# A four-layer image network on one core: a fixed order for the attention's keys, bounded scores in the linear attention, and gate scores from raw tokens

## The chip, the cores and the metric

The kernel runs on one core of one Trainium2 chip, in float32, as one launch. The metric is the device time of that core in microseconds (us). The kernel before was run three times: 7568.02 us is the median, 7562.25 the lowest and 7576.92 the highest.

The core has five engines that each run their own stream of instructions. In the profile they are PE (the matrix engine; PEld is its loading of weights), DVE (vector), ACT (activation functions), POOL (GpSimd) and SP, which here only issues transfers. Transfers (DMA) between the device memory and the on-chip memory run beside them. An engine waits for another on semaphores. Matrix products land in PSUM, [...]from which ACT or DVE copies ("evicts") them.

## What is computed

The input is 8 images of 56 x 56 pixels with 128 channels. Four layers follow one another; tokens are the 3136 pixels of an image.

```python
x = conv_layer(x)                  # layer 0: deformable convolution, layer norms, MLP
x = whiten(x)                      # layer 1: channels decorrelated by a 64 x 64 matrix
t = x.reshape(8, 3136, 128)
# layer 2: 8 heads of 16, keys = queries = values = h
h = ln(t) @ W_k.T
t = t + softmax(h @ h.T / 4) @ h @ W_o.T          # per image and head
t = t + ffn(ln(t))
# layer 3: linear attention, 4 heads of 32
q, k, v = split(ln(t) @ w_in.T)
q = softmax(q, over the 32 of a head) / sqrt(32)
k = softmax(k, over all 25088 tokens)             # one softmax for each channel
ctx = k.T @ (v / N)                               # per head, 32 x 32
t = t + ln((ctx applied to q) @ w_out.T + b_out) * ln_w
t = t + ffn(ln(t))

def ffn(x):                        # 64 experts, each picks 8 tokens of each image
    logits = x @ gate_w.T + gate_b                # [3136, 64]
    probs = softmax(logits, over the tokens)
    vals, idx = top_k(probs of each expert, 8)
    pooled = sum of the 8 chosen tokens, weighted by vals
    out = gelu([pooled, 1] @ weight1), then [.., 1] @ weight2
    return scatter_add(out * vals at idx)
```

`ln` subtracts a token's mean over its 128 channels and multiplies by one over the root of its variance plus a small constant.

## The kernel before

An image's 3136 tokens are worked in 28 tiles of 112 tokens (T = 112, NT = 28), four tiles to a group (GT = 4, 448 columns, QC), seven groups to an image (NG = 7), so 56 groups over all images. Channels lie on 128 partitions where a matrix is "transposed" (names with a T), tokens lie on partitions otherwise. Everything runs in the order of the functions that `token_layers` (L2223) calls, after layers 0 and 1.

*Weights* (L2241 to L2274). Weight matrices are loaded and transposed on PE. `gate_weights` (L2210) does this for the two gates, those of layer 2 and layer 3.

*`attention_keys`* (L1038) works image by image. It loads the tokens (L1061), stores them by token into `tok` (L1062), makes mean and variance of each tile (`bn_stats` and `bn_aggr` on DVE, L1066 and L1067) and one over the root with `rsqrt` (L1134: an addition on DVE at L1139, a power on POOL at L1140). It normalizes each tile on DVE (`xn`, L112), transposes it on PE (L121) and copies the transposed group with ACT (L122) into `xT`. Fourteen products `p_h` (L1082) give the keys, evicted by turns by ACT (L1086) and DVE (L1090) into `kT`; 25 products `p_v` (L1097) give the values, evicted into `va` (L1105, L1107). Keys and values are stored in device memory. A last step squares the values on POOL (`sq`, L1116) and reduces them on DVE (L1118, L1119), for a bound of all scores. Its instructions are ordered by the framework's scheduler, which picks for each engine among what is ready.

*`query_bound`* (L2079) makes a bound of layer 3's query scores from the norms of 128 rows of weights: `low3` is its negative and `small3` a flag that says whether it is below a limit (`SMALL3`, 40). A similar flag, `small`, chooses between `attend` and a version for large scores. Both flags are read into registers (`values_load`) before a branch.

*`attend`* (L1154) is layer 2's attention and the longest part, with an order written out by hand. Scores `p_s` (L1251), exponentials (L1259) and products with the values (L1304) run over blocks of queries. When a block's sums `acc` are complete, `finish` (L1343) divides them, multiplies by `wo_pad` on PE (L1374), adds the tokens (L1385), makes statistics (L1390), normalizes, transposes (`p`, L1411) and makes the gate scores `pr` (L1416). `finish` is a Python generator: each `yield` is a place where its issue pauses and other work is put in. Behind the last scores, at L1489 to L1497, the generators still open are advanced, two of them (`later[:2]`) in turn. `choose` (L1654) then picks the 8 best tokens of each expert from `pr`.

*Experts of layer 2* (`run_experts`, L2314) follow.

*`context_sums`* (L1947) is the softmax of layer 3's keys, over all tokens, times the tokens themselves. `pipeline` (L1934) advances one generator per group by one `yield` in each turn and starts a new group each turn, so several groups are in flight in different phases. A group's statistics come from `group_stats` (L2013); `minus_mean` (L2024) makes `ms`, and `scale_shift` (L2030) normalizes with four ACT instructions (L2033). Then the group is transposed, the keys `p_k` are made by channel, the running maximum over the groups so far is updated (`ntop`, L1983 to L1985), the factor by which the old sums fall is made (`fall`, L1987), the exponentials (`eT`, L1992) are transposed back on PE (`p_e`, L1997), copied by DVE (`e`), and multiplied with the tokens (`p_x`, L2002); `tot` and `den` (L2004, L2005) take the group in.

*`context_weights`* (L2038) turns the sums into one 128 x 128 matrix `cw`.

*`linear_layer`* (L2106) has a similar pipeline over the 56 groups: queries `p_q` and their exponentials `q`, the sum over each head `m` (DVE, L2146) and the division (POOL, L2148), a transposition, the product `p_y` with `cw` (L2155), its squares (ACT, L2161), one over the root of their mean (L2165 on DVE, L2166 on POOL), `y` (DVE, L2169), the addition to the tokens (POOL, L2172), and, for the feed-forward part, statistics, `ms`, normalization on ACT, a transposition (`nT`) and the gate scores (`p_g`, L2187). After the seventh group of an image, `choose` runs in the same pipeline. `context_sums` and `linear_layer` are ordered by the scheduler. The experts of layer 3 end the kernel.

Of the kernel before, what the change touches and what calls it, by code (L numbers as in the profile page):

```python
# [8 lines left out]
F32 = mybir.dt.float32  # L9
I32 = mybir.dt.int32  # L10
# [1027 lines left out]
def attention_keys(tc, k, w, yv, tok, kT_out, va_out, low, small):  # L1038
# [5 lines left out]
    n_b = yv.shape[1]  # L1044
    with ExitStack() as ctx:
        cp = ctx.enter_context(tc.tile_pool(name="akc", bufs=1))
        bp = ctx.enter_context(tc.tile_pool(name="akb", bufs=2))
        ps = ctx.enter_context(tc.tile_pool(name="akp", bufs=6, space=PSUM))
        vas = []
# [8 lines left out]
        for n in range(n_b):  # L1058
            t_sb = bp.tile([T, NT, C], F32, name="t")
            for h in range(2):  # L1060
                nc.sync.dma_start(t_sb[h * IW : (h + 1) * IW], yv[h, n])  # L1061
            nc.sync.dma_start(tok[n].rearrange("(t p) c -> p t c", p=T), t_sb)  # L1062
# [5 lines left out]
            rs = rsqrt(nc, k, bp, mv, NT)  # L1068
            xT = bp.tile([C, S], F32, name="xT")
            for g in range(NG):  # L1070
                xn = bp.tile([T, GT, C], F32, name="xn")
                for i in range(GT):
                    normalize(nc, xn[:, i], t_sb[:, g * GT + i], mv, rs, g * GT + i)
                transpose_group(
                    nc, k, ps, "m", xT[:, g * QC : (g + 1) * QC], xn, nc.scalar.copy
                )
            kT = bp.tile([128, 2, S], F32, name="kT", bufs=1)
            for g in range(2):
                for c in range(NG):
# [5 lines left out]
                    if c % 2:  # L1085
                        nc.scalar.activation(  # L1086
                            kT[:, g, cols], p, AF.Identity, bias=w.one16, scale=DK**-0.25
                        )
                    else:
                        nc.vector.tensor_scalar(  # L1090
                            kT[:, g, cols], p, DK**-0.25, w.one16, ALU.mult, ALU.add
                        )
                nc.sync.dma_start(kT_out[n, g], kT[:, g])
            va = vas[n % 2]
# [15 lines left out]

            sq = bp.tile([128, 2 * KT * 4, DK], F32, name="sq", bufs=1)
            v = va.rearrange("p g t j d -> p (g t j) d")[:, :, :DK]
            nc.gpsimd.tensor_tensor(sq, v, v, ALU.mult)  # L1116
            top = bp.tile([128, 2 * KT * 4], F32, name="top")
            nc.vector.tensor_reduce(top, sq, AX.X, ALU.add)  # L1118
            nc.vector.tensor_reduce(tops[:, n : n + 1], top, AX.X, ALU.max)  # L1119
# [1267 lines left out]
```

## Time and profile before

| part of the profiled execution | us from the span's start |
|---|---|
| layers 0 and 1, weights | 0 to 1515 |
| `attention_keys` | 1520 to 1869 |
| `attend`, all engines in full work | 1869 to 6397 |
| `attend`, its end | 6397 to 6480 |
| experts of layer 2 | 6480 to 6663 |
| `context_sums` | 6656 to 6909 |
| `linear_layer` | 6915 to 7345 |
| experts of layer 3 | 7345 to 7566 |
| span of the profiled execution | 7566.5 |
| its time | 7568.32 |
| median of three runs | 7568.02 |

The profile is of one execution, and the runs show how far another may lie from it. The whole span has PE busy 6499.5 us (86%), DVE 5210.3 (69%), ACT 4198.0 (55%) and POOL 2941.4 (39%). Such shares are averages over stages with different limits, so a stage is read from its own stretch of the timeline. In a line of the timeline stand start, duration, engine, line of the code, operation, output and inputs with their shapes, how many instructions were drawn together, and in square brackets how long the engine was idle before and what it waited for.

### The profile page before, as it was taken

The numbers are of one execution on the slowest core, as the hardware profiler recorded it, in microseconds if no ns is written. First come the engines' busy times: TensorE is split into PE (matmuls) and PEld (weight loads), VectorE is DVE, ScalarE is ACT, GpSimd is POOL, SyncE is SP. The second block draws the span as 40 slices with busy tenths as digits, with TensorE's granted clock in tenths as the row PEclk, the third lists the DMA queues.
The fourth block names the chain that finished last, engine by engine and source line by source line (L and its number), as shares of the span: only waits on it lengthen the run. The fifth ranks groups of instructions, "written<-read, shape, count | busy, mean of one in ns | idle before, by whom it ended". The sixth has DMA issues, their size and how long they took to land. (4 is left out here: it accounts for less than half of the span.)

```text
span 7566.5 us, 158564 instructions
## 1 busy us (share of the span) xinstructions
PE 6499.5 (86%) x60063; PEld 2893.4 (38%) x60063; DVE 5210.3 (69%) x9787; ACT 4198.0 (55%) x6563; POOL 2941.4 (39%) x2557
## 2 busy tenths in 40 slices
PE   7859999656999999999999999999999999556764
PEld 5646666433333323323323323323333323245542
DVE  7866664366677777777777777777777777356761
ACT  5634444222766666666666666666666665156750
POOL 0011111122544444444444444444444444333763
PEclk9968989866999999999999999999999999789776
DMA  6544343476888778778778778778778777544544
GB/s 162 163 101 88 85 87 63 155 224 202 198 202 205 188 187 205 190 185 205 192 186 205 189 185 206 187 189 205 191 186 206 187 185 170 202 109 125 134 132 139
DMA packets 737876, 1287.44 MB, mean 170 GB/s; under 512 B 119042, under 2 KB 504452, under 8 KB 730308
## 3 DMA queue, kind: packets, MB, share of 16 engines
q1 hardware_dynamic: 726868, 1260.77, 65.9%
q0 software_dynamic: 6144, 12.60, 0.6%
q8 instruction: 486, 7.96, 0.5%
q10 hardware_dynamic: 4080, 3.68, 0.2%
q14 instruction: 298, 2.44, 0.1%
HBM read 286.04 MB, written 197.81 MB: 64 GB/s over the span
## 5 line engine op out<-in xcount | busy, mean ns | idle before, releaser
L1259 ACT ACTIVATE e<-p_s 128x768 f32<-128x768 f32 (+2 forms) x3712 | 2887.7, 830 | 1577.2 <-PE p_s L1251 1312.7
L1297 POOL COPY x<-sq 32x1152 f32<-32x1152 f32 x1792 | 2062.4, 1151 | 2008.8 <-PE p_s L1251 1240.1
L1270 DVE STREAM_TRANSPOSE sq<-e 128x768 f32<-128x768 f32 x2688 | 2433.8, 950 | 516.7 <-ACT e L1259 267.0
L1251 PE MATMUL p_s<-q,kT 32*128 32x384 f32 (+2 forms) x14848 | 1893.4, 547 | 41.1 <-ACT e L1259 23.3
L1304 PE MATMUL av<-e,va 128*32 128x384 f32 (+2 forms) x14848 | 1644.2, 515 | 13.5 <-DVE acc L1327 8.5
L1304 PE MATMUL avx<-x,va 128*32 128x384 f32 x10752 | 1129.5, 492 | 57.5 <-issue 36.9
L1251 PEld LDWEIGHTS p_s<-q,kT 32*128 32x128 f32 (+1 forms) x14848 | 649.9, 180 | 1265.8 <-issue 836.1
L1304 PEld LDWEIGHTS av<-e,va 128*32 128x32 f32 (+1 forms) x14848 | 293.6, 108 | 1028.7 <-issue 938.6
L1304 PEld LDWEIGHTS avx<-x,va 128*32 128x32 f32 x10752 | 351.8, 111 | 635.8 <-issue 597.4
L616 POOL TENSOR_TENSOR rs<-rs,mhalf 112x4 f32<-112x4 f32 x112 | 116.0, 1036 | 786.2 <-DVE rs L615 786.2
L1323 DVE TENSOR_TENSOR acc<-acc,avx 128x384 f32<-128x384 f32 x336 | 183.7, 547 | 232.3 <-PE avx L1304 227.7
L121 PE MATMUL p_tr<-ident,xn 112*128 112x112 f32 x672 | 132.9, 337 | 184.0 <-DVE xn L112 138.3
L1140 POOL TENSOR_TENSOR rs<-rs,mhalf 112x4 f32<-112x4 f32 (+2 forms) x136 | 167.9, 1235 | 243.6 <-DVE ntop L1985 123.9
L532 ACT COPY wT<-p_w 88x448 f32<-88x448 f32 x152 | 138.1, 923 | 197.8 <-PE p_w L530 159.4
L2033 ACT ACTIVATE xn<-t,ms,rs 112x128 f32<-112x128 f32 x448 | 185.2, 487 | 73.8 <-DVE ms L2026 73.7
L644 PE MATMUL p_f<-x1T,w 128*128 128x448 f32 x448 | 206.1, 584 | 4.4 <-DVE x1T L639 2.8
L121 PEld LDWEIGHTS p_tr<-ident,xn 112*128 112x128 f32 x672 | 97.3, 167 | 278.2 <-issue 184.9
L530 PE MATMUL p_w<-ident,wide 112*88 112x112 f32 x896 | 144.6, 300 | 62.7 <-DMA px<-strips 37.8
L1393 POOL TENSOR_TENSOR rs_b<-rs_b,mhalf 128x3 f32<-128x3 f32 (+1 forms) x72 | 58.5, 815 | 352.8 <-DVE rs_b L1392 350.2
L327 DVE SCALAR_TENSOR_TENSOR acc<-xp,dw,acc 128x3136 f32<-128x3136 f32 x48 | 166.5, 3470 | 37.6 <-ACT acc L322 37.3
L628 DVE TENSOR_TENSOR y<-y,p_rs 128x448 f32<-128x448 f32 x112 | 69.2, 618 | 176.7 <-PE p_rs L621 176.6
L122 ACT COPY xT<-p_tr 128x448 f32<-128x448 f32 x112 | 59.6, 532 | 224.8 <-PE p_tr L121 198.7
(366 smaller groups left out, 7904.0 us busy)
## 6 DMA issues: line engine op xcount, KB each, us to landing
x<-sq SPq DMA_DIRECT2D x5376, 144.0 KB
w<-in_L_ffn_weight_dram SPq DMA_DIRECT2D x64, 1024.0 KB
px<-strips SPq DMA_DIRECT2D x64, 616.0 KB
va_d<-va SPq DMA_DIRECT2D x16, 1600.0 KB
xT_d<-xT SPq DMA_DIRECT2D x112, 224.0 KB
xT<-xT_d SPq DMA_DIRECT2D x112, 224.0 KB
kT_d<-kT SPq DMA_DIRECT2D x16, 1568.0 KB
t<-t_a SPq DMA_DIRECT2D x16, 1568.0 KB
```

The costliest lines, as they stand in the source:

```text
L121: nc.tensor.transpose(p[:, i, :], src[:, i, :], k.ident[:T, :T])
L327: nc.vector.scalar_tensor_tensor(acc, xp[:, j // 3 : j // 3 + IH, j % 3 : j % 3 + IW], dw[:, j : j + 1], acc, ALU.mult, ALU.add,)
L530: nc.tensor.transpose(p[:, g], around[:, :, g], k.ident[:T, :T])
L644: nc.tensor.matmul(p, q.w1[:, f * 128 : (f + 1) * 128], x1T, start=True, stop=True)
L1140: nc.gpsimd.tensor_tensor(rs, rs, k.mhalf[:m, :n], ALU.pow)
L1251: nc.tensor.matmul(ss[j // 2][:m, j % 2, :width], kT[rows, 128 * i : 128 * i + m], q[rows, :width], start=True, stop=True,)
L1259: nc.scalar.activation(e[:m, 2 * j : 2 * j + 2, :width], ss[j][:m, :, :width], AF.Exp)
L1270: nc.vector.transpose(sq[:, :, i, j : j + 2].rearrange("p s j c -> p j s c"), exps[u, b, a, i][:, j : j + 2, :QB].rearrange("p j (s c) -> ...
L1297: nc.gpsimd.tensor_copy(*moves.pop(0))
L1304: nc.tensor.matmul(out, keys[u, b][1][:m, i, j, :], e[j], start=start, stop=stop)
L1323: nc.vector.tensor_tensor(to, to, in_order(av), ALU.add)
L2033: nc.scalar.activation(out[:, i], x[:, i], AF.Identity, bias=ms[:, i : i + 1], scale=rs[:, i : i + 1])
```

## The change

Six things are changed.

1. `attention_keys` gets an order written out by hand (`manual_schedule`: each engine runs its instructions in the order of the program). A tile's partitions become half and row of the image, with 28 pixels of the row in one partition, so that a load or store moves 14336 bytes in one piece instead of 512. The statistics of the next image are a generator that is advanced between the key products. ACT evicts all keys. The transposed group is copied into `xT` at places 28 columns apart. The squares and reductions of an image are issued in the next one.
2. At the end of `attend` all open generators are advanced in each round, three such rounds begin while the last squares are still being worked, and the buffers that several blocks need at once are the score squares' or more in number.
3. `context_sums_bounded` is new. Instead of the running maximum it subtracts the bound; it has an order written out by hand, makes keys by token, and sums in one PSUM tile over all groups. A column of ones beside the tokens gives the denominators. The flag `small3` chooses between it and the old function.
4. `query_bound` becomes `score_bound`, over 256 rows (queries and keys), and stands ahead of the weights.
5. In `linear_layer` the gate scores are made from tokens that are not normalized, by token, and multiplied by one over the root of the variance; then they are transposed.
6. For that, the gates' weights are centred: each row's mean is subtracted, so that a token's mean adds nothing. This is done for both gates.

```diff
-def attention_keys(tc, k, w, yv, tok, kT_out, va_out, low, small):
+def attention_keys(tc, k, w, y, tok, kT_out, va_out, low, small):
...
+        def statistics(n):
             t_sb = bp.tile([T, NT, C], F32, name="t")
-            for h in range(2):
-                nc.sync.dma_start(t_sb[h * IW : (h + 1) * IW], yv[h, n])
-            nc.sync.dma_start(tok[n].rearrange("(t p) c -> p t c", p=T), t_sb)
+            inner = tok[n].rearrange("(h f i) c -> f h i c", f=2, i=NT)
+            for f in range(2):
+                of = slice(f * IH, (f + 1) * IH)
+                nc.sync.dma_start(t_sb[of], y[:, n, f * NT : (f + 1) * NT])
+            yield
+            for f in range(2):
+                nc.sync.dma_start(inner[f], t_sb[f * IH : (f + 1) * IH])
...
             for i in range(NT):
                 nc.vector.bn_stats(st[:, i], t_sb[:, i])
                 nc.vector.bn_aggr(mv[:, i], st[:, i])
-            rs = rsqrt(nc, k, bp, mv, NT)
+                if i % GT == GT - 1:
+                    yield
+            stats[n] = t_sb, mv, rsqrt(nc, k, bp, mv, NT)
...
+        for n in range(n_b):
+            t_sb, mv, rs = stats.pop(n)
+            if n + 1 < n_b:
+                ahead.append(statistics(n + 1))
+                advance(ahead)
...
+                p = ps.tile([C, GT, 2, IH], F32, tag="m", name="p_tr")
+                for i in range(GT):
+                    nc.tensor.transpose(
+                        p[:, i].rearrange("c f h -> c (f h)"), xn[:, i], k.ident[:T, :T]
+                    )
+                nc.scalar.copy(by_place[:, g * GT : (g + 1) * GT], p)
+            advance(tail)
...
                         p, wk[:, g * 128 : (g + 1) * 128], xT[:, cols], start=True, stop=True
                     )
-                    if c % 2:
...
+                    advance(ahead)
+                    nc.scalar.activation(
+                        kT[:, g, cols], p, AF.Identity, bias=w.one16, scale=DK**-0.25
+                    )
```

The end of `attend`, and the scores' bound:

```diff
+        ending = True
+        rooms = [room()]
+        early = 3
         while jobs:
             keep_squares()
+            if early:
+                go_on_all()
+                early -= 1
             from_squares()
-        for work in urgent:
-            go_on(work)
-        ending = True
+            while urgent:
+                go_on(urgent.pop(0))
+        while urgent:
+            go_on(urgent.pop(0))
+        rooms.append(room())
         while later:
-            for work in later[:2]:
-                go_on(work)
+            go_on_all()
...
-def query_bound(tc, k, w, w_in, low, small):
+def score_bound(tc, k, w_in, low, small):
...
-        raw = bp.tile([C, C], F32, name="raw")
-        nc.sync.dma_start(raw, w_in[:C])
+        raw = bp.tile([C, 2, C], F32, name="raw")
+        nc.sync.dma_start(raw, w_in[: 2 * C].rearrange("(a p) c -> p a c", p=C))
```

The new function for the context sums, from its first yield on, with the branch:

```diff
+            rs, mv = group_stats(nc, k, wp, t)
+            yield
+            ms = minus_mean(nc, wp, rs, mv)
+            xn = wp.tile([T, GT, C + 1], F32, name="xn", bufs=6)
+            nc.gpsimd.memset(xn[:, :, C:], 1.0)
+            for i in range(GT):
+                if i % 2:
+                    nc.scalar.activation(xn[:, i, :C], t[:, i], AF.Identity, ...)
+                else:
+                    nc.vector.tensor_scalar(xn[:, i, :C], t[:, i], ...)
+            yield
+            p = ps.tile([C, GT, T], F32, tag="m", name="p_tr")
+            for i in range(GT):
+                nc.tensor.transpose(p[:, i], xn[:, i, :C], k.ident[:T, :T])
+            xT = wp.tile([C, QC], F32, name="xT")
+            nc.scalar.copy(xT, p.rearrange("c a t -> c (a t)"))
+            nc.sync.dma_start(xT_out[n][:, g * QC : (g + 1) * QC], xT)
+            yield
+            p = ps.tile([T, GT, C], F32, tag="m", name="p_k")
+            for i in range(GT):
+                nc.tensor.matmul(p[:, i], xT[:, i * T : (i + 1) * T], w.w_in[:, C : 2 * C], ...)
+            e = wp.tile([T, GT, C], F32, name="e")
+            nc.scalar.activation(e, p, AF.Exp, bias=low[:T])
+            yield
+            for i in range(GT):
+                nc.tensor.matmul(sums, e[:, i], xn[:, i], ...)
...
-        context_sums(tc, k, w, t_a, xT_d, tot, den)
+        with tc.If(taken > 0) as both:
+            context_sums_bounded(tc, k, w, low3, *sums)
+        with both.Else():
+            context_sums(tc, k, w, *sums)
```

The linear layer and the gates:

```diff
-            rs, mv = group_stats(nc, k, wp, t)
-            yield
-            ms = minus_mean(nc, wp, rs, mv)
-            xn = wp.tile([T, GT, C], F32, name="xn")
-            scale_shift(nc, xn, t, rs, ms)
+            rs, _ = group_stats(nc, k, wp, t)
+            tT = wp.tile([C, QC], F32, name="tT")
+            transpose_group(nc, k, ps, "m", tT, t, nc.scalar.copy)
...
-            nT = wp.tile([C, QC], F32, name="nT")
-            transpose_group(nc, k, ps, "m", nT, xn, nc.scalar.copy)
+            p = ps.tile([T, GT, E], F32, tag="m", name="p_g")
+            for i in range(GT):
+                nc.tensor.matmul(
+                    p[:, i], tT[:, i * T : (i + 1) * T], gate_w, start=True, stop=True
+                )
+            sc = wp.tile([T, GT, E], F32, name="sc")
+            nc.vector.tensor_tensor(
+                sc, p, rs.unsqueeze(2).to_broadcast([T, GT, E]), ALU.mult
+            )
             yield
-            p = ps.tile([E, QC], F32, tag="m", name="p_g")
-            nc.tensor.matmul(p, gate_w, nT, start=True, stop=True)
+            p = ps.tile([E, GT, T], F32, tag="m", name="p_sc")
+            for i in range(GT):
+                nc.tensor.transpose(p[:, i], sc[:, i], k.ident[:T, :T])
...
+    mean = rp.tile([E, 1], F32, name=name + "_m")
+    nc.vector.tensor_reduce(mean, raw, AX.X, ALU.add)
+    nc.vector.tensor_scalar(mean, mean, 1.0 / C, None, ALU.mult)
+    nc.vector.tensor_scalar(raw, raw, mean, None, ALU.subtract)
```

## The prediction

> **What bounds the kernel now.** I read the slices of the page first, then a table of busy time by stretch with the bounds of each stage (columns: stretch, its length, then busy time of PE, PEld, DVE, ACT and POOL, granted clock, DMA share, GB/s), then the timeline of one repetition of each stage.
>
> ```profile
> PE   7859999656999999999999999999999999556764
> PEclk9968989866999999999999999999999999789776
> ...
> 1532.70:1868.90 336.20, 200.79 (x854) 133.25 (x854) 226.58 (x820) 85.69 (x200) 78.25 (x16) 0.71 0.66 217
> 1869.00:6397.00 4528.00, 4364.20 (x41547) 1429.55 (x41547) 3423.48 (x4905) 2922.62 (x3818) 2145.24 (x1890) 0.98 0.80 194
> 6410.90:6455.00 44.10, 23.11 (x85) 14.36 (x85) 25.53 (x78) 0.00 (x0) 4.28 (x5) 0.65 0.14 41
> 6656.00:6909.00 253.00, 169.90 (x1008) 122.92 (x1008) 172.17 (x841) 167.47 (x448) 62.20 (x62) 0.92 0.38 104
> 6915.00:7345.00 430.00, 285.75 (x1580) 210.71 (x1581) 316.74 (x1160) 303.13 (x1016) 279.91 (x264) 0.77 0.54 142
> 1598.00:1606.00 8.00, 0.00 (x0) 0.00 (x0) 5.03 (x12) 0.00 (x0) 3.18 (x2) 0.50 1.01 421
> ```
>
> The main part of `attend` takes 4528 us with PE busy for 4364 of them: full, and its code unchanged. The four other stretches (keys, end of `attend`, context sums, linear layer) have no full engine. Each is a chain that passes from engine to engine, and all of the change is there. The keys of one image show such a chain, with the first tokens still to be loaded:
>
> ```profile
> 1564.13 4.80 POOL L1140 TENSOR_TENSOR rs<-rs,mhalf 112x28 f32<-112x28 f32 x1
> 1569.50 7.00 DVE L112 TENSOR_SCALAR xn<-t,mv,rs 112x128 f32<-112x128 f32 x27
> 1578.16 11.18 PE L1082 MATMUL p_h<-xT,wk 128*128 128x448 f32 x26
> 1589.17 5.89 PE L1097 MATMUL p_v<-wkT,xT 128*128 128x128 f32 x50
> ```
>
> POOL's power, DVE's normalizing, PE's keys and values come one after another; normalizing begins at 1532.7 for the first image and the last value copy ends at 1853.1: 320.4 us, a period of 42.1 us an image after 25.7 for the first.
>
> [...] the granted clock is 0.50 in 1574 to 1580 and 1.00 from 1582 on, and 0.71 over the stage. [...] `ms` takes 0.86 us in the linear layer, where POOL is busy, and 0.16 in the context sums.
>
> **Keys.** The new order makes the statistics of image n+1 while image n's keys are multiplied. DVE per image: 28 normalizations x 0.256 = 7.2 us; the deferred reductions 3.48 + 0.35 = 3.9; 28 pairs of statistics. In a fixed order each pair waits for itself; the end of `attend` shows it (first two rows before's keys, last two there):
>
> ```profile
> 1520.57 0.26 DVE L1066 BATCH_NORM_STATS2 st<-t 112x6 f32<-112x128 f32 x1
> 1520.83 0.26 DVE L1066 BATCH_NORM_STATS2 st<-t 112x6 f32<-112x128 f32 x1
> ...
> 6418.06 0.29 DVE L1390 BATCH_NORM_STATS2 st<-t 128x6 f32<-128x128 f32 x1
> 6418.49 0.26 DVE L1390 BATCH_NORM_STATS2 st<-t 128x6 f32<-128x128 f32 x1
> ```
>
> About 0.39 us a pair instead of 0.26: 28 x 0.39 = 10.9. The square of the values is 5.5 on POOL and is now beside DVE. The load of n+1 stands on SP's queue behind n-1's value stores: 3.3 MB at 421 GB/s (the last stretch above) is 7.8 us, [...]: it lands about 13 us after the image began. From there 10.9 + the add 0.3 + POOL 4.8 + handovers put the next image's first normalization at 29 to 30. PE's own path is 7.2 + 1.6 + 14 x 0.75 [...] + 5.9 = 27[...]. ACT now has all 14 key copies (14 x 0.63 = 8.9) and strided copies at 0.93 (like L558's 128x448 copy; 0.53 contiguous): 15.4 + value copies, inside 30. So a period of 30 (26.5 if the load lands early [...], 34 if it is late): 7 x 30 + 26 = 236 against 320.4, -84. Behind the stage two loads of flags go (1865.1 to 1868.9 holds them) as the bound moves ahead of the weights, -3; the bound's own chain there costs +1. **-86** (-110 to -58). Centring both gates is six small operations in that preparation, inside the +1.
>
> **End of `attend`.** From the last `acc` (6410.9) to the last `pr` (6455.0) pass 44.1 us with DVE busy 25.5: five blocks finish two by two. Now all go on in each step, and three early rounds take some of it beside the last squares. That moves about 10 us of DVE's 25.5 ahead, leaving 15.8 + some 5 of stalls; PE's order then lets output matmuls stand before the last `avx` until DVE has transposed, +9. 15.8 + 5 + 9 = 29.8: **-15** (-22 to -6). The square tiles it re-uses are free by then, so no store waits.
>
> **Context sums.** 55 periods from 6676.4 to 6904.5: 4.15 us, 4.25 in the steady part. What goes: the maximum 0.61, its two helpers, the copy of `e` 0.68, `tot` 0.32, `den` 0.20 on DVE; `fall` 0.29 and half of the 4 x 0.41 normalizations on ACT; 4 transposes (0.65) on PE. What comes: two normalizations on DVE (0.52), a `memset` on POOL, keys as four matmuls of 128 columns (about 1.1). What stays is a loop that a fixed order lays bare:
>
> ```profile
> 6673.60 0.15 DVE L1139 TENSOR_SCALAR rs<-mv 112x4 f32<-112x4 f32 x1
> 6673.83 1.01 POOL L1140 TENSOR_TENSOR rs<-rs,mhalf 112x4 f32<-112x4 f32 x1 [1.07 <-DVE rs L1139]
> 6674.87 0.16 DVE L2026 SCALAR_TENSOR_TENSOR ms<-mv,rs 112x4 f32<-112x4 f32 x1 [0.79 <-POOL rs L1140]
> ```
>
> From `rs` to `ms` 1.27 us. In program order DVE waits there with the next group's statistics behind it: 0.16 + 0.52 + 4 x 0.39 + 0.16 + about 1.2 = 3.6 a group. PE's turn is 1.16 + 1.1 + 0.55 + 0.45 = 3.3, ACT's 0.82 + 0.53 + 0.65 = 2.0. So (4.25 - 3.6) x 56 = -36, and +3 for the second pair of branches (flag loads at the linear layer take 6909.5 to 6914.7 for one). **-33** (-47 if the POOL wait is covered by PE's turn of 3.3 and both are short; -10 if 4.0).
>
> **Linear layer.** 6.42 us a group on average, 5.37 where no `choose` runs. Its loop there, in which the next `y` waits for POOL:
>
> ```profile
> 7127.01 1.13 DVE L2169 SCALAR_TENSOR_TENSOR y<-p_y,rs,ln_w 112x128 f32<-112x128 f32 x4 [1.13 <-POOL rs L2166]
> 7130.80 0.39 DVE L2165 TENSOR_SCALAR rs<-sq 112x4 f32<-112x4 f32 x1
> 7131.33 1.02 POOL L2166 TENSOR_TENSOR rs<-rs,mhalf 112x4 f32<-112x4 f32 x1 [0.17 <-DVE rs L1139]
> 7132.38 0.87 DVE L2169 SCALAR_TENSOR_TENSOR y<-p_y,rs,ln_w 112x128 f32<-112x128 f32 x3 [1.12 <-POOL rs L2166]
> ```
>
> What goes: `ms` 0.86 from DVE in this loop, four normalizations (1.66) from ACT. What comes: the product `sc` from PSUM (112x256, estimated at 0.35 to 0.5 from the 0.68 of the 128x448 copy), four gate matmuls and four transposes on PE (about +1, PE has 144 us idle here). POOL remains with two powers, a product and an add, 1.05 + 1.02 + 1.01 + 1.27 = 4.35 a group, so it becomes the bound at 4.4 to 4.8. `choose` (+1.05 a group) is the same. -0.6 x 56 = **-34** (-60 to 0).
>
> **Sum.** -86 - 15 - 33 - 34 = -168; 7568.3 - 168 = **7400**. The profiled execution was 7568.32 (span 7566.5), the median of the runs 7568.02: the same.
>
> **Rivals.** The keys stay at 35 us because the load stands exposed behind the value stores: for it, 421 GB/s is all that the queue moves and the load is issued behind 3.3 MB; against it, all 14 steps of the keys lie after its landing. -86 becomes -50: about 7437. The linear layer doesn't shrink, since its scheduler puts the new product where `ms` was and POOL at 4.35 has little left to give: 7434. Better than forecast: keys at 26.5 (-24) and context sums at 3.2 (-22), 7354. The change doesn't do what it says where the bound of layer 3 exceeds 40: 256 rows of 128 weights drawn with variance 1/128 have a largest squared norm near 1.4, so the bound is sqrt(1.01 x 128 x 1.4) = 13.5; else 7436. On the slower side, one mechanism: the granted clock in the attention stage. It is 0.98 there, and PE fills it. If that clock falls as gaps elsewhere close, 4364 us stretch in proportion; from 0.943 (4364 x (0.98/0.943 - 1) = 171) it outweighs all the gains, and at 0.93 it gives +235: 7635. Nothing in the profile shows a dependence of one stage's clock on another's, so this is unlikely.
>
> **How the numbers follow.** Forecast 7400: 0.62; keys at 35: 0.13; linear unchanged: 0.12; better: 0.08; bound not taken: 0.02; clock: 0.03. The range 7352 to 7460 takes in the first five, and half of each of the two shortfalls at once. A measurement of this kernel tells 0.2%, 15 us, from no change; even all the small ends together give -74, so faster 0.96, same 0.01, slower 0.03.
>
> **What would show it.** First `xn` of two successive images 30 us apart (35 or more: the load, seen as DVE waiting on DMA); last `acc` to last `pr` near 30; one `p_tr` to the next in the context sums 3.6; `y` to `y` 4.8 outside `choose`; the attention stage 4528 within 10 at clock 0.98. The forecast is wrong if the stage lengths are right in sum only by chance, or if the attention stage moves by more than 15.

## The result: 1.2% faster, half of what was forecast

The changed kernel takes 7480.44 us (median of four runs, 7476.04 to 7491.99) against 7566.61 us for the kernel before (four runs on the same chips). The ratio is 0.9879, with a 95% interval from 0.9861 to 0.9897. That is 86 us; 168 were forecast, and the forecast range ended at 7460.

The profiled execution of the changed kernel has a span of 7490.2 us, 76.3 below the 7566.5 before. Cut at events that both traces have, the difference falls into these parts:

| part, from event to event | before | after | difference | forecast |
|---|---|---|---|---|
| start to the last store of `y` (layers 0, 1; unchanged) | 1501.5 | 1506.6 | +5.1 | 0 |
| to the first key load of `attend` | 367.4 | 317.8 | -49.6 | -86 |
| to the last product `av` (unchanged) | 4528.8 | 4546.4 | +17.6 | 0 |
| to the last gate score `pr` of `attend` | 56.7 | 37.8 | -18.9 | -15 |
| to the first `xn` of the context sums | 218.6 | 215.9 | -2.7 | 0 |
| to their last product | 235.5 | 221.6 | -13.9 | -33 |
| to the last `pr` of the linear layer | 416.1 | 403.1 | -13.0 | -34 |
| to the end | 241.8 | 240.9 | -0.9 | 0 |

Two lines are marked as unchanged code. All kernels of this study share the attention's code, and in the profiles of the changed ones the attention from its first to its last `av` took between 4514.1 and 4535.2 us (4513.4 before, 4530.6 after). So +17 is no more than one execution and another differ by, and the stages that were changed are read from the trace, not from the total.

The granted clock goes with these differences. The profile prints 0.98 for all, but the mean of the trace's clock records over this stretch is 0.9849 before and 0.9818 after. PE's busy 4360.2 us before, stretched by 0.9849 / 0.9818, become 13.8 more, and after it is busy for 4374.0. Over all 20 kernels the clock there runs from 0.9803 (`l_hand`, 4535 us) to 0.9855 (`c_turn`, 4514 us). One profile of the kernel before can't tell whether the change itself adds some us here.

The slices of the page after (tenths of the span, PE's busy share and the granted clock):

```profile
PE   7858999767999999999999999999999999556764
PEclk9968988877999999999999999999999999789877
```

And the busy time of the stretches (stretch, length, busy PE, PEld, DVE, ACT, POOL, granted clock, DMA share, GB/s): keys, attention, end of the attention, context sums, linear layer.

```profile
1541.30:1824.40 283.10, 215.45 (x851) 138.48 (x851) 225.52 (x749) 151.09 (x264) 77.69 (x16) 0.77 0.71 254
1840.20:6370.80 4530.60, 4373.46 (x41539) 1430.49 (x41539) 3425.08 (x4902) 2919.09 (x3814) 2144.99 (x1891) 0.98 0.79 193
6389.80:6409.20 19.40, 13.54 (x49) 6.88 (x49) 15.34 (x46) 0.00 (x0) 2.59 (x3) 0.76 0.14 41
6606.00:6846.50 240.50, 153.93 (x1120) 132.60 (x1120) 134.44 (x673) 106.74 (x225) 69.87 (x123) 0.94 0.40 111
6865.00:7265.00 400.00, 282.76 (x2132) 261.79 (x2132) 288.49 (x1143) 225.33 (x792) 276.97 (x263) 0.84 0.53 144
```

The end of the attention did what it should (19.4 us from the last `acc` to the last `pr`, DVE busy for 15.3 of them). Keys, context sums and linear layer still have no engine that is full. In the keys DVE is "busy" for 225 of 283 us, as many as before, although it no longer copies keys.

In the keys, the timeline of image 3 of the kernel after shows where the forecast of 30 us an image went (start, duration, engine, line, operation, in brackets the idle time before and its cause):

```profile
1641.01 12.54 DVE L112 TENSOR_SCALAR xn<-t,mv,rs 112x128 f32<-112x128 f32 x28
1641.26 5.53 POOL L1093 TENSOR_TENSOR sq<-va 128x3200 f32<-128x3200 f32 x1 [1.25 <-DVE va L1148]
1653.47 3.47 DVE L1096 TENSOR_REDUCE top<-sq 128x200 f32<-128x3200 f32 x1
1655.13 13.43 PE L1126 MATMUL p_h<-xT,wk 128*128 128x448 f32 x28 [1.08 <-ACT xT L1119]
1659.31 0.29 DVE L1081 BATCH_NORM_STATS2 st<-t 112x6 f32<-112x128 f32 x1 [1.97 <-DMA t<-y]
1670.75 4.79 POOL L1175 TENSOR_TENSOR rs<-rs,mhalf 112x28 f32<-112x28 f32 x1 [23.96 <-DVE rs L1174]
1675.59 12.47 DVE L112 TENSOR_SCALAR xn<-t,mv,rs 112x128 f32<-112x128 f32 x28
```

The period, from the first `xn` of an image to that of the next, is 34.6 us, not 30. Two things stand in it that the forecast hadn't. First, the 28 normalizations take 12.5 us instead of 7.2, and the 5.3 too many are the 5.53 us in which POOL squares the values. Second, the next image's tokens land 18.3 us after the image began, not 13; from there 11 us of statistics and 4.8 of POOL's power lead to the next `xn`.

The first was to be seen before. Two lines of the kernel before, which the prediction passed over:

```profile
1558.49 5.52 POOL L1116 TENSOR_TENSOR sq<-va 128x3200 f32<-128x3200 f32 x1 [25.84 <-DVE va L1107]
1559.06 4.99 DVE L1139 TENSOR_SCALAR rs<-mv 112x28 f32<-112x28 f32 x1
```

An addition on 28 numbers in each partition takes 0.18 us elsewhere; here it took 4.99 and ended when POOL's squares ended (1564.05 and 1564.01). In the kernel after, one of the 28 normalizations above does the same: it takes 5.61 us, where their median is 0.34, and ends at 1646.87, POOL's squares at 1646.79. By what means the squares hold DVE up, no run shows. The prediction had seen a small operation take 0.86 us instead of 0.16 where POOL is busy, but it didn't price the 5.5 us of the largest POOL instruction of the stage, which the new order puts beside the normalizations.

The second was to be seen there too. Behind the stores of 1598 to 1606, from which the prediction took its 421 GB/s, the kernel before loads the next tokens, in pieces of 512 bytes, and from 1608 to 1616 next to nothing else moves:

```profile
DMA packets 2733, 1.41 MB, mean 176 GB/s; under 512 B 22, under 2 KB 2731, under 8 KB 2731
...
q1 hardware_dynamic: 2732, 1.40, 97.0%
```

That is 176 GB/s, with the transfer engines 97% busy (the last line). The 421 was the rate of key and value stores.

### The profile page after: what moved, and what is told of

Same layout as the page of the kernel before. It is cut to its first block, busy times and chain, and to the rows that moved or that the text cites. A ratio compares the mean times of both kernels' runs of the same rounds, so it can differ in the third digit from the quotient of the medians.

```text
span 7490.2 us, 159591 instructions
## 1 busy us (share of the span) xinstructions
PE 6502.9 (87%) x60735; PEld 2959.3 (40%) x60735; DVE 5149.8 (69%) x9565; ACT 4125.0 (55%) x6180; POOL 2942.2 (39%) x2613
## 5 line engine op out<-in xcount | busy, mean ns | idle before, releaser
L1339 PE MATMUL av<-e,va 128*32 128x384 f32 (+2 forms) x14848 | 1648.1, 516 | 13.9 <-DVE acc L1362 8.5
L649 PE MATMUL p_f<-hid,w 128*128 128x448 f32 x448 | 179.0, 542 | 0.0
L2166 DVE BATCH_NORM_STATS2 st<-t 112x6 f32<-112x128 f32 x448 | 115.7, 269 | 86.2 <-POOL t L2322 53.1
L645 ACT ACTIVATE hid<-p_f,b 128x448 f32<-128x448 f32 x224 | 136.8, 637 | 60.0 <-PE p_f L644 52.3
L530 PEld LDWEIGHTS p_w<-ident,wide 112*88 112x88 f32 x896 | 118.7, 172 | 111.4 <-issue 78.0
```

The costliest lines, as they stand in the source:

```text
L530: nc.tensor.transpose(p[:, g], around[:, :, g], k.ident[:T, :T])
L649: nc.tensor.matmul(p[:, :QC], q.w2[:, f], hid[:, f], start=(f == 0), stop=(f == 3))
L1339: nc.tensor.matmul(out, keys[u, b][1][:m, i, j, :], e[j], start=start, stop=stop)
```

## The experiments

Each run is given with its ratio to the kernel before, from runs on the same chip. The chips differed a little (the kernel before took 7567 to 7577 us), so kernels are compared by their ratios, and by stages of their traces. Periods in the keys are means over the last five of the seven. Landing is when the next image's statistics begin, counted from the first `xn` of one image in the middle; from image to image it differs by up to 2 us.

### Keys: two edits, alone and together

The squares moved behind the next image's normalizations, by a small POOL copy that waits for the last `xn`:

```diff
         def largest(n):
...
+            yield
+            if last:
+                nc.gpsimd.tensor_copy(after_xn, last.pop()[:, GT - 1, :1])
             nc.gpsimd.tensor_tensor(sq, v, v, ALU.mult)
-            yield
```

> Only the squares of the values on POOL are moved behind the last normalization of the next image. Theory 1 (the squares stop DVE's normalization, and this alone is what the keys lost against the forecast): xn takes 7.2 us instead of 12.5, the period of an image falls from 34.5 to about 30, the whole by 30 us to 7450. Theory 2 (the tokens of the next image land 18.3 us after an image began, so statistics and POOL's power end as late as before): xn takes 7.2 us, but DVE then waits for the load, the period stays at 34 to 34.5, the whole at 7476 to 7480.

Ratio 0.9900 (0.9884 to 0.9917). `xn` fell to 7.25 us, so the squares did hold DVE up. The period didn't fall: 36.7 us. The load landed 18.8 us after the image began, and the statistics began there. As the reduction now stands behind the later squares, nothing was gained in front of it either. The copies of the values stand behind the statistics on DVE, and PE's last value products waited for them:

```profile
1677.06 6.40 PE L1143 MATMUL p_v<-wkT,xT 128*128 128x128 f32 x28 [5.47 <-DVE va L1153]
```

So a late load now held PE up as well, and the period is above both expectations. Theory 1 falls as a sole cause.

The second half of each load on ACT's queue:

```diff
-                nc.sync.dma_start(t_sb[of], y[:, n, f * NT : (f + 1) * NT])
+                queue = nc.scalar if f else nc.sync
+                queue.dma_start(t_sb[of], y[:, n, f * NT : (f + 1) * NT])
```

> Only the second half of each token load is issued by ACT's queue instead of SP's, so that the two halves, on different partitions, move side by side and not behind the value stores. Theory 1 [...]: the load lands sooner, nothing else changes, period 34.5, 7480. Theory 2 [...]: PE's chain 12.5 + 1 + 13.3 + 6.9 = 33.7 remains, period about 34, 7475. A third theory (the load alone is the cause): period 30, 7450.

Ratio 0.9892 (0.9875 to 0.9908), period 34.4 us. The edit missed its aim: the load landed at 18.2 us, in the kernel after at 18.3.

> Both edits at once. Theory 2 (two chains of equal length, each hiding the other): period 29 to 30, the whole falls by 31 to 38 us to about 7445, more than the two single edits together. Theory 1: the same as the squares alone.

Ratio 0.9884 (0.9868 to 0.9901), period 36.0, landing at 18.7. That is near the squares alone, as theory 1 has it. It doesn't speak against two chains, since the load wasn't made earlier; the next two parts try that in other ways.

### Keys: the rate of the token load

In the trace of the kernel after, 2 us of value stores (1645 to 1647) and 2 us of token loads (1651 to 1653):

```profile
DMA packets 84, 0.87 MB, mean 435 GB/s; under 512 B 16, under 2 KB 16, under 8 KB 16
...
DMA packets 28, 0.40 MB, mean 201 GB/s; under 512 B 0, under 2 KB 0, under 8 KB 0
...
q1 hardware_dynamic: 28, 0.40, 96.0%
```

The load moves at 201 GB/s, with the transfer engines 96% busy (the last line). The forecast's 13 us leave it some 5 us behind the 7.8 of the stores, for 1.6 MB about 310 GB/s: that was its author's estimate, and no trace showed it. One transfer over 112 partitions instead of two over 56:

```diff
-            for f in range(2):
-                of = slice(f * IH, (f + 1) * IH)
-                nc.sync.dma_start(t_sb[of], y[:, n, f * NT : (f + 1) * NT])
+            nc.sync.dma_start(t_sb, y[:, n].rearrange("h (f i) c -> h f i c", f=2))
...
-        by_place = xT.rearrange("c (h f i) -> c i f h", f=2, i=NT)
+        by_place = xT.rearrange("c (p i) -> c i p", i=NT)
```

> Only the place of a token in its tile: partition = 2 x row + half instead of half x 56 + row, so that each load and each store of the tokens is one transfer over 112 partitions instead of two over 56. Theory A (a transfer over 56 neighbouring partitions moves at half the rate, 200 GB/s, whatever the length of its pieces): the load moves at 350 GB/s or more and lands about 14 us after an image began instead of 18.3; [...] the period stays at 33.5 to 34.5. Theory B [...]: it lands at 18 us as before, period 34.5. Both: 7490 on this chip, within 10.

Ratio 0.9882 (0.9865 to 0.9898), period 34.8, landing at 19.3. Theory A falls for the load, which stayed at 0.37 to 0.42 MB in 2 us. The token store, in the same layout, moved 0.65 MB in 2 us. So it isn't the 56 partitions that make the load slow.

> The same, and the squares on POOL behind the last normalization of the next image, and their reduction on DVE one image later still, where DVE waits for the load. Theory A with two chains of equal length: normalization 7.2, load lands at 14, statistics 11 to 25, power to 30: period 30 to 31, the whole 25 to 31 us less than the single edit, about 7463. Theory B: the load at 18.3, period 34.5 to 35.5, no gain.

Ratio 0.9886 (0.9869 to 0.9902), period 36.2, landing at 18.8: no gain, as theory B. With the same layout and the load in seven pieces:

```diff
-            nc.sync.dma_start(t_sb, y[:, n].rearrange("h (f i) c -> h f i c", f=2))
+            for g in range(NG):
+                part = y[:, n].rearrange("h (f i) c -> h f i c", f=2)
+                of = slice(g * GT, (g + 1) * GT)
+                nc.sync.dma_start(t_sb[:, of], part[:, :, of])
```

> As the kernel with one transfer over 112 partitions and later squares, but each token load is cut into seven, of 4 pixels (2048 bytes) for each partition. Theory C (a piece of 14336 bytes written into one partition moves at half the rate): the load moves at 330 GB/s or more, lands at 14 us, period 31. Theory D (the rows of the source, 229376 bytes apart, are what halves the rate): still 200 GB/s, the last piece lands at 18 to 19 us, but statistics of the first groups may begin earlier: period 32 to 34.

Ratio 0.9826 (0.9805 to 0.9846), period 30.3. The statistics began 13.7 to 15.0 us after the image in the middle images, since they need only the first piece. The rate rose little (0.40 to 0.48 MB in 2 us), so theory C doesn't carry it. Theory D had the rate, and too long a period; no run moved the rows of the source, so its cause isn't shown. Why this load moves at half the rate of the value stores stays open; that it needn't land as a whole is what gained here.

### Keys: the load out of the way

A third token buffer, the load issued one image earlier:

```diff
+        def load():
+            n = len(loaded)
+            if n < n_b:
+                t_sb = bp.tile([T, NT, C], F32, name="t", bufs=3)
...
         for n in range(n_b):
             t_sb, mv, rs = stats.pop(n)
+            load()
```

> The tokens are loaded one image earlier (a third buffer), all else as in the changed kernel. Theory 2 (two chains of equal length: the load with statistics and power, and PE's chain [...]): DVE no longer waits for the load, but PE's chain of 12.5 + 1 + 13.3 + 6.9 = 33.7 remains: period 33.7, 5 us less in all. If the load alone had been the cause: period 29, 35 us less.

Ratio 0.9866 (0.9849 to 0.9883), period 34.1: DVE no longer waits for a load, and PE's chain, which begins with the `xn` beside the squares, holds the period, as theory 2 has it.

> Tokens one image earlier, and the squares on POOL behind the last normalization of the next image, their reduction one image later. Theory 2: both chains are shortened, DVE's to 7.2 + 3.9 + 11 + 5.1 = 27.2, PE's to 28.4, transfers to about 28: period 28.5 to 29.5, some 36 us less than the changed kernel. If transfers of 9.7 MB need more than 30 us an image: 31 to 33.

Ratio 0.9832 (0.9815 to 0.9849), period 28.9; from the last store of `y` to the attention's first load 281.1 us instead of 317.8. Its timeline, the same image:

```profile
1654.82 7.25 DVE L112 TENSOR_SCALAR xn<-t,mv,rs 112x128 f32<-112x128 f32 x28
1661.99 3.48 DVE L1107 TENSOR_REDUCE top<-sq 128x200 f32<-128x3200 f32 x1
1665.64 5.52 POOL L1104 TENSOR_TENSOR sq<-va 128x3200 f32<-128x3200 f32 x1 [3.25 <-DVE top L1107]
1665.78 0.28 DVE L1089 BATCH_NORM_STATS2 st<-t 112x6 f32<-112x128 f32 x1
1676.96 0.18 DVE L1191 TENSOR_SCALAR rs<-mv 112x28 f32<-112x28 f32 x1
1677.22 4.80 POOL L1192 TENSOR_TENSOR rs<-rs,mhalf 112x28 f32<-112x28 f32 x1 [6.05 <-DVE rs L1191]
1683.26 6.99 DVE L112 TENSOR_SCALAR xn<-t,mv,rs 112x128 f32<-112x128 f32 x27
```

From one `xn` to the next 28.4 us, of which PE is busy for 26.3 and the transfer engines for 94%. The squares still run beside DVE, but beside the statistics, and these aren't held up: the 28 pairs took 11.2 us (1665.78 to 1676.96), as in the kernel after (1659.31 to 1670.49). So the squares hold up some DVE operations (the normalizations, 12.54 us instead of 7.25, and the small addition, 4.99 instead of 0.18) and not the statistics. With this the keys are settled: two chains of about 34 us lay side by side. Without the load's, the period fell by 0.5 us; without the squares beside `xn`, it rose by 2; without both, it fell by 5.7.

### Context sums: one more turn

```diff
             rs, mv = group_stats(nc, k, wp, t)
             yield
+            yield
             ms = minus_mean(nc, wp, rs, mv)
```

> Only the context sums: one more turn between a group's statistics and its normalization, so that DVE has the next group's statistics to do while POOL makes the power. Theory 1 (DVE's wait of 1.2 us for POOL in every group sets the period of 3.94): DVE's turn is 1.79 + 0.2 + 0.2 + 0.7 = 2.9 and PE's 2.85, so the period falls to about 3.0 and the whole by 50 us to 7430. Theory 2 (the hand-overs along PE's turn set it, as its waits for xn and e suggest): the period stays at 3.7 to 3.9, the whole at 7468 to 7480.

Ratio 0.9819 (0.9803 to 0.9835). The period is 2.93 us where no load is waited for, and the `rs` of the first group to that of the last takes 171.5 us instead of 216.3. The stage as cut in the table takes 183.9 us instead of 221.6: theory 1. The kernel after, one group:

```profile
6720.73 0.17 DVE L1174 TENSOR_SCALAR rs<-mv 112x4 f32<-112x4 f32 x1
6721.05 1.01 POOL L1175 TENSOR_TENSOR rs<-rs,mhalf 112x4 f32<-112x4 f32 x1 [2.88 <-DVE rs L1174]
6722.09 0.16 DVE L2174 SCALAR_TENSOR_TENSOR ms<-mv,rs 112x4 f32<-112x4 f32 x1 [1.19 <-POOL rs L1175]
6722.88 0.29 DVE L2166 BATCH_NORM_STATS2 st<-t 112x6 f32<-112x128 f32 x1
6724.67 0.17 DVE L1174 TENSOR_SCALAR rs<-mv 112x4 f32<-112x4 f32 x1
```

The same lines with the further turn:

```profile
6748.22 0.17 DVE L1174 TENSOR_SCALAR rs<-mv 112x4 f32<-112x4 f32 x1 [0.39 <-ACT xn L2110]
6748.30 0.15 DVE L2175 SCALAR_TENSOR_TENSOR ms<-mv,rs 112x4 f32<-112x4 f32 x1
6748.54 1.01 POOL L1175 TENSOR_TENSOR rs<-rs,mhalf 112x4 f32<-112x4 f32 x1 [1.88 <-DVE ms L2175]
6749.08 0.28 DVE L2167 BATCH_NORM_STATS2 st<-t 112x6 f32<-112x128 f32 x1
6751.15 0.17 DVE L1174 TENSOR_SCALAR rs<-mv 112x4 f32<-112x4 f32 x1 [0.39 <-ACT xn L2110]
```

In the first, DVE stands idle for 1.19 us in each group, because the next thing in its order needs what POOL is making. In the second, `ms` follows `rs` at once: it is that of an older group, and POOL's power runs beside the next normalization.

### Linear layer

The layer as it was before, in the changed kernel:

> The linear layer of the kernel before in the changed kernel; all else as changed. Theory 1 (the new gate scores save time only in the first groups, before the first choice, 0.8 us for each of 8, and behind the last): the whole rises by 10 to 15 us against the changed kernel, an image with a choice takes 49.2 us in both. Theory 2 (they save in every group, and another part takes it back): the rise is 30 or more.

Ratio 0.9897 (0.9880 to 0.9913), which doesn't tell it from the changed kernel. In the trace, everything behind the attention took 1093.8 us instead of 1081.6: 12 us, as theory 1. The `t` additions on POOL (one for each group) show why. In the first groups, before a first choice of tokens, they come every 4.58 us after and every 5.37 before. But from one choice (`best`) to the next an image takes 49.2 us after, and 49.2 before. Two lines of each kind, before and then after:

```profile
6967.15 1.28 POOL L2172 TENSOR_TENSOR t<-t,y 112x512 f32<-112x512 f32 x1 [0.26 <-DVE y L2169]
6972.52 1.28 POOL L2172 TENSOR_TENSOR t<-t,y 112x512 f32<-112x512 f32 x1 [0.26 <-DVE y L2169]
7090.76 3.41 DVE L1659 MAX8 best<-pr 64x8 f32<-64x3136 f32 x1
7139.94 3.41 DVE L1659 MAX8 best<-pr 64x8 f32<-64x3136 f32 x1
...
6904.14 1.27 POOL L2322 TENSOR_TENSOR t<-t,y 112x512 f32<-112x512 f32 x1
6908.72 1.28 POOL L2322 TENSOR_TENSOR t<-t,y 112x512 f32<-112x512 f32 x1
7013.94 3.41 DVE L1718 MAX8 best<-pr 64x8 f32<-64x3136 f32 x1
7063.13 3.41 DVE L1718 MAX8 best<-pr 64x8 f32<-64x3136 f32 x1
```

From the second choice to the last, six of the eight images, the new gate scores saved nothing (286.9 us, 285.2 before).

The layer in program order:

```diff
         ps = ctx.enter_context(tc.tile_pool(name="llp", bufs=8, space=PSUM))
+        ctx.enter_context(
+            tc.manual_schedule(
+                engines={
+                    e.engine for e in (nc.tensor, nc.scalar, nc.vector, nc.gpsimd, nc.sync)
+                }
+            )
+        )
```

> Only the linear layer: its instructions run in the order of the program on each engine instead of the scheduler's. Theory 1 (in the images with a choice of tokens the order in which DVE and POOL wait for each other sets the 49.2 us of an image, since neither is busy for more than 37 of them): in program order everything a turn reads was made a turn before, DVE has 4.6 us a group and 9.5 for a choice, so an image takes 42 to 45 us and the whole falls by 30 to 45 us. Theory 2 (a resource that the profile doesn't show busy, such as the transfers of the tokens, sets 49.2): an image stays at 49.

Ratio 0.9895 (0.9879 to 0.9912); 49.7 us an image, and 1102.2 us behind the attention instead of 1081.6. It is slower, theory 1 falls. In one image of the kernel after DVE is busy for 37.1 us, and in this order for 42.8; pairs of statistics that follow one another 0.40 us apart are a part of that. Then three of four gathers left out:

```diff
-    for c in range(NC):
+    for c in range(1 if few else NC):
         gather(nc, x[:, c], t_in, rows[:, c : c + 1])
```

> The linear layer in program order, and of the four gathers of a choice only one is left (three fourths of the chosen tokens are replaced by the first fourth). Theory 3 (bursts of a choice on POOL and DVE add to the period, because each of the two has no more than a turn's work ahead of the other): an image with a choice takes 3 x 1.25 = 3.75 us less than the 49.7 of the program order, the whole about 26 less than that kernel. Theory 2 (a resource that isn't shown sets 49): 49.5, no change.

Ratio 0.9897 (0.9874 to 0.9919), 50.1 us an image: theory 3, as priced, falls too. The gathers lie beneath something else. A choice put behind the groups' work of each turn:

```diff
-                yield from choose(nc, k, wp, ps, pr, t_out[n], taken[:, n], pooled[:, n])
+                late.append(
+                    choose(nc, k, wp, ps, pr, t_out[n], taken[:, n], pooled[:, n])
+                )
...
+            advance(flight, len(flight))
+            advance(late, len(late))
```

> The linear layer in program order, and in each turn the instructions of a choice behind those of the groups instead of ahead of them. Theory 4 (a choice's own chain of hand-overs from DVE to PE to DVE to POOL stands in front of the groups' work on every engine, and the gathers were hidden beneath it): a choice then costs only its busy time on DVE, an image falls from 49.7 to 44 to 47 us, the whole to 20 to 40 us below the kernel in program order. Theory 2 (a resource that isn't shown): an image stays at 49 to 50.

Ratio 0.9889 (0.9868 to 0.9911), 49.5 us: theory 4 falls in program order. But its trace names waits (lines of the timeline, with the idle time before each in brackets):

```profile
7025.65 2.02 PE L2288 MATMUL p_q<-w_in,xT 128*112 128x128 f32 x8 [4.61 <-DMA xT<-xT_d]
7031.31 0.30 ACT L1726 ACTIVATE found<-best,ntop 64x8 f32<-64x8 f32 x1 [2.86 <-DVE ntop L1723]
7037.31 0.69 PE L1780 MATMUL p_pool<-expert,chosen 128*128 128x64 f32 x2 [4.68 <-DVE chosen L112]
7040.84 1.04 POOL L1785 DMA_INDIRECT chosen<-t_c,rows  x1 [2.68 <-DVE rows L1744]
```

Each is an instruction of a choice, or the first of a group, and all that stands behind it in the order of its engine waits too.

> The same late choice, with the scheduler's order kept as in the changed kernel. Theory 4, if the scheduler ranks by the order of the program: an image below 47 us, 15 to 25 us in all. If the scheduler ranks by its own estimate of times: an image stays at 49.2, no change.

Ratio 0.9866 (0.9840 to 0.9891), 47.9 us an image: between the two expectations. In the trace the layer took 395.2 us instead of 403.1, but what follows it 246.8 instead of 240.9: some 2 us in all, and the ratio doesn't tell it from the changed kernel. Last, a turn between all hand-overs of a choice, and the transposed tokens loaded a turn earlier:

```diff
+def choose_in_turns(nc, k, wp, ps, pr, t_in, taken, pooled):
...
+    nc.vector.tensor_copy(found[:, 0], at)
+    yield
...
+    for c in range(NC):
+        normalize(nc, x[:, c], x[:, c], mv, rs, c)
+    yield
+    p = ps.tile([C, E], F32, tag="m", name="p_pool")
...
             nc.sync.dma_start(xT, xT_in[n][:, g * QC : (g + 1) * QC])
             yield
+            yield
```

> The linear layer in program order with the choice late, and now every hand-over of a choice from one engine to another has a turn between (DVE to PE, PE to DVE, DVE to POOL, DVE to ACT; the gathers two by two), and a group's transposed tokens are loaded a turn earlier. Theory 5 (several hand-overs of a choice inside one turn hold the in-order engines up: PE waited 4.7 us for the chosen tokens, POOL 2.7 for their rows, ACT 2.9 for the maximum): an image falls from 49.5 to DVE's own work, 44 to 47, the whole 20 to 40 us below the kernel in program order. Theory 2: an image stays at 49 to 50.

Ratio 0.9856 (0.9833 to 0.9878), 47.6 us an image, 1067.5 us behind the attention: 35 less than in program order without it, 14 less than the changed kernel. Theory 2 falls, since 49 can be undercut without touching a resource. Theory 5 holds for the whole; the image stayed above its 44 to 47. The two edits weren't tried one by one. In one image of 47.5 us DVE is now busy for 42.1. What is left was not isolated.

### Together

> The tokens one image earlier with later squares, and the further turn in the context sums. The two are in different stages, so the gains add: 36 + 50 us below the changed kernel, about 7395, ratio to the kernel before 0.977.

Ratio 0.9776 (0.9757 to 0.9795): 7407.89 us against 7576.28. Keys and context sums add up as expected.

> The same, with the linear layer in program order and the choice late. If theory 4 holds, a further 15 to 30 us below: about 7370. If it doesn't: 10 to 15 us above the one without it.

Ratio 0.9801 (0.9782 to 0.9820): the intervals overlap, but in the traces all behind the attention takes 1076 us against 1045, slower, as the case without theory 4 had it.

> The fastest kernel so far (tokens an image earlier with later squares, a further turn in the context sums) with that linear layer. Theory 5: 15 to 30 us below it, about 7385 where the kernel before takes 7576. Theory 2: 10 to 20 us above it.

Ratio 0.9757 (0.9737 to 0.9777): 7392.40 us against 7570.76. It is the fastest kernel here, 2.4% below the kernel before; the changed kernel is 1.2% below. From the one without the linear layer's turns its interval doesn't part it; in the traces the stretch behind the context sums takes 635.2 us against 646.7.

## Why the prediction was wrong, point by point

- **Keys, -86 forecast, -49.6 measured.** Two terms of the sum failed, and each alone would have been enough (34.1 us with the squares beside `xn` alone, 36.7 with the late load alone). "28 normalizations x 0.256 = 7.2" was 12.5, since POOL's squares were said to be "now beside DVE" at no cost: beside the statistics they cost nothing, beside the normalizations 5.3 us. And "it lands about 13 us after the image began" was 18.3, since the load ran at 201 GB/s and not at the estimate. The seven periods, 237.6 us for 7 x 30, hold 27.6 of the 36 us that were missed; the rest lies before the first `xn` and behind the last. The first rival (35 us, the load exposed) had the right period, and one of its two causes; it priced the whole at 7437 because it kept the other three stages as forecast.
- **The fixed order's price, 0.39 us for a pair of statistics, PE's path of 27:** right, to 0.40 us and about 28.4. Of the 27, about 2 us are for products at the lower clock: in the kernel before, a key product took 0.954 us at a granted clock of 0.50 (1576 to 1580) and 0.539 at 1.00 (from 1582 on). With both obstacles gone the period was 28.9, so the transfers fit inside 30 too.
- **End of the attention, -15:** -18.9. The working held: 19.4 us for its 15.8 + 5, and PE's extra wait, priced at 9, was 5.8. That wait lies before the last `acc` (13.2 us behind the last `av` before, 19.0 after), so "last `acc` to last `pr` near 30" was the wrong sign to look for.
- **Context sums, -33:** -13.9. The mechanism, DVE standing in its order for POOL's power, was right, and the further turn showed it. Two sizes were off. The turn was summed as 3.6 and measured 3.94: four pairs took 1.79 us from the first to the next `rs` instead of 1.56, and hand-overs around `ms` and `xn` 0.1 more. And the old period was set at 4.25 for all 56 groups, although 4.15 was the average that the prediction gave itself: (4.15 - 3.94) x 55 = 12.
- **Linear layer, -34:** -13.0. "-0.6 x 56" carried the gain of the groups without a choice (5.37 to 4.58 measured, POOL 4.35 and the bound, as forecast) to all 56. In the images with a choice, "`choose` (+1.05 a group) is the same" failed: its cost grew by what the groups had saved. Why an image comes out equal to 0.1 us stays open; the order of a choice's hand-overs, with the earlier load, is worth 1.6 of its 49.2. The rival that kept this layer at its old time was nearer.
- **The attention's clock** was to stay at 0.98 and the stage within 10 of 4528. The stage moved by 17.6, more than the 15 that the prediction named as a sign of being wrong, with the clock 0.3% lower and PE busy for 13.8 us more. That is what the slower rival describes, in a small size. It isn't shown to come from the change: with more gaps closed, the first kernel under "Together" had 0.9845 and 4519 us.

## What to carry to other kernels

When an order is changed, ask for the largest instruction of POOL which DVE instructions will now run beside it, and look in the trace of before for a small DVE instruction that ends when POOL's ends: here 4.99 us instead of 0.18 told of the 5.3 us that the normalizations lost. Two chains of the same length hide each other, so an experiment that takes away one shows nothing, and both must be taken away before either is called harmless. A rate measured in one stretch belongs to that stretch and to its kind of transfer (421 GB/s for stores, 176 for the token load behind them): look for the same load in the trace of before; a gain measured in groups without a burst doesn't multiply by all groups.

## What was not expected of the hardware

- A load of 14336-byte rows moved at 201 GB/s with the transfer engines nearly always busy (96% in the stretch shown), and cutting it into 2048 bytes or spreading it over 112 partitions brought no more than 242. In 512-byte pieces, in the kernel before, it moved at 176. Token stores with rows of the same size moved at 323 GB/s, and value stores at 435.
- Beside POOL's squares (5.53 us), 28 of DVE's normalizations took 12.54 us instead of 7.25 and a small addition 4.99 instead of 0.18; the addition, and the one normalization that was long (5.61 us), ended within 0.1 us of the squares. 28 pairs of statistics beside the same squares took their usual 11.2 us.
- The same attention code took 4514 to 4535 us in single profiled executions, at mean clocks of 0.9855 to 0.9803: the longer ones mostly had the lower clock.
